# Batch norm's mean taken from column sums of the adjacency, in a four-layer graph network on one core

## The chip, the cores and the metric

The kernel runs on one core of a Trainium2 chip. The metric is the device time of one execution in microseconds. A core has five engines that each work through a list of instructions of their own: PE (matrix products), DVE (vector work), ACT (activations and copies), POOL (here mostly indirect DMAs, which gather or scatter rows by a list of indices) and SP (here only DMA issues). They wait for each other by semaphores.

## What is computed

The inputs are x, 2708 nodes with 128 features, and adj, 2708 x 2708 with about 0.6% of its entries set and a full diagonal. Four layers follow each other; around each there is a residual sum and a layer norm.

```python
# layer 0
msg = adj.T @ x
inv_deg = 1.0 / adj.sum(axis=0)            # 0 where that is infinite
x = layernorm(x + msg * inv_deg[:, None])
# layer 1
s = x @ msg_w[:, :D].T;  d = x @ msg_w[:, D:].T
messages = gelu(s[:, None, :] + d[None, :, :] + msg_b)
aggregated = einsum('ijd,ij->id', messages, adj)
new = concatenate([x, aggregated], -1) @ upd_w.T + upd_b
x = layernorm(x + layernorm(gelu(new) + x) * ln_w + ln_b)
# layer 2
h = adj @ (x @ W) + b
mean = h.mean(axis=0);  var = ((h - mean) ** 2).mean(axis=0)
h = gamma * (h - mean) * rsqrt(var + EPS) + beta
x = layernorm(x + where(h >= 0, h, 0.2 * h))
# layer 3: attention with four heads over the neighbours, then a product with w
```

Layer 0 sums adj over its rows for each column. Layer 2's mean is a mean of h over the nodes.

## The kernel before, in words

**Blocks.** The nodes are cut into 22 blocks: 21 of P = 128 and one of 20. `quads()` (L324) groups them for vector work into five groups of four, one of one and the last of 20 rows.

**Layer 0 (L343 to L808).** `load(b)` (L392) brings the rows of a block of adj on SP's queue. `count_and_sum` multiplies them with x, which has a column of ones behind its 128 features, so that the accumulators `accs0` hold adj.T @ x and, in column D of each block, the column sum of adj (L406). Meanwhile DVE extracts up to 31 entries for each row (`extract`, L421). DVE's order in this part is written out by hand (`manual_schedule`, L343); the other engines' orders, and DVE's later, come from a scheduler that puts instructions in order by their dependencies and estimates of their time. Nodes are then ranked by their number of entries, so that blocks in ranked order have nodes of like count (`rank`, `perm`).

The column sums are copied into `deg` (L701 to L711), zeros are replaced and the reciprocal taken. The generator `layer0(b0, count, n)` (L719) then works on a group of blocks: it normalises x + msg/deg into slot 1 of the tile `dx`, [128, count, 2, 128] (L754), transposes it on PE, multiplies it by the second half of msg_w and copies the product into slot 0 (L773). `d_dram` gets slot 0 in natural order (L774, SP). `dx_dram` gets both slots, 256 floats for each node, scattered to the node's rank: one indirect DMA on POOL for each block (`scatter`, L253).

**Layers 1 and 2 (L812 to L1005).** A loop runs over TURNS (L974), the ranked blocks in a fixed order. In a turn, `own_row` (L818) loads the block's 256 columns of `dx_dram` into `x_s`, on SP's queue, one turn ahead (L821). `messages` (L827) transposes it (L832), copies it to `x_st` on ACT (L833), and makes the node's own term on PE (L834, L835). DVE adds that to slot 0 (L849), ACT takes the Gelu. Then POOL gathers neighbours' rows of d_dram, up to eight to a buffer of `msg`, of which there are five (L245, L856). DVE adds (L858), ACT takes the Gelu (L861), and DVE weighs and sums (L844, L846) into `parts`. `update` (L868) has products for the new features (L872, L881 to L883), ACT's Gelu, two layer norms that go between DVE and ACT, a scatter to x2_dram, a transposition (L899), and the product with layer 2's W, which is copied into `xw` (L904). `x_b`, x_s plus a bias, is made on DVE at L877. Beside these, `transposed` (L906) transposes blocks of adj on PE (L931), copies them on ACT (L936) and stores them to at_dram (L938, SP).

From turn 11 on, with two blocks to a turn, `layer2(k)` (L950) gathers 128 rows of at_dram by `perm` on POOL and adds 22 products into six PSUM banks `accs2`, one for each output block of 128 columns (L957). Block 20 and block 21 lie in the first half of bank 5; its columns 2D to 4D aren't used. The last block follows behind the loop.

**Batch norm (L1030 to L1080).** DVE adds b to each group from PSUM into `hb` (L1052); PE multiplies a matrix of ones with each block, which sums over the nodes into `ps_m` (L1054). Two small products of weights for layer 3 follow on DVE (`w_prod`, L1060 to L1062). The mean is a scaled copy of ps_m (L1065); DVE subtracts it from every group (L1069), ACT squares (L1070), PE sums the squares into `ps_v` (L1072), and `scale` is made of it (L1077 to L1080). `masks` (L1085) makes index masks for layer 3 on DVE. The normalise loop (L1118) then multiplies by scale (L1120), adds beta, goes through the leaky relu, the residual and the layer norm, and stores tables for layer 3.

**Layer 3 (L1174 to L1508)** gathers rows of those tables and works on DVE, PE and ACT in orders written out by hand.

Of the kernel before, what the change touches and what calls it, by code (L numbers as in the profile page):

```python
# [9 lines left out]
FP = mybir.dt.float32  # L10
AF = mybir.ActivationFunctionType
ALU = mybir.AluOpType
# [3 lines left out]
P = 128  # L16
N = 2708
D = 128
NFULL = N // P
NREM = N - NFULL * P  # L20
NBLK = NFULL + 1
# [64 lines left out]
def gnn_resnorm_kernel(  # L86
# [21 lines left out]
    nc = tc.nc  # L108

    const = ctx.enter_context(tc.tile_pool(name="const", bufs=1))  # L110
    ident = const.tile([P, P], FP, name="ident")
# [98 lines left out]
    lists_dram = tables.tile([NBLK * P, LW], FP, name="lists_dram")  # L210

    d_dram = tables.tile([NBLK * P, D], FP, name="d_dram")
    dx_dram = tables.tile([NBLK * P, 2 * D], FP, name="dx_dram")
    at_dram = tables.tile([NBLK * P, N], FP, name="at_dram")
    x2_dram = tables.tile([NBLK * P, D], FP, name="x2_dram")

# [20 lines left out]
    ones = keep.tile([P, P], FP, name="ones")  # L237
# [6 lines left out]
    def gather(dst, table, index):  # L244
        nc.gpsimd.indirect_dma_start(  # L245
            out=dst,
            out_offset=None,
            in_=table[0:N, :],
            in_offset=bass.IndirectOffsetOnAxis(ap=index, axis=0),
        )  # L250
# [73 lines left out]
    def quads():  # L324

        parts = [(b, 4) for b in range(0, 20, 4)] + [(20, 1), (21, 1)]
        return [(b, c, BLOCKS[b + c - 1][1]) for b, c in parts]
# [7 lines left out]
    with ExitStack() as layer:  # L335
# [373 lines left out]
        tails = work.tile([P, 4], FP, name="tails")  # L709
        nc.vector.tensor_copy(tails[0:NREM], accs0[1][0:NREM, 3 * (D + 1) : 3 * (D + 1) + 4])  # L710
        nc.vector.tensor_copy(deg[0:NREM, NFULL : NFULL + 1], tails[0:NREM, 3:4])  # L711
        nc.vector.tensor_scalar(zero, deg, 0.0, None, ALU.is_equal)
        nc.vector.tensor_tensor(deg, deg, zero, ALU.add)
        nc.vector.reciprocal(deg, deg)
# [4 lines left out]
        def layer0(b0, count, n):  # L719
            h = brief.tile([P, 4, D], FP, name="h0", bufs=5)  # L720
            sums = brief.tile([P, 4], FP, name="sums0", bufs=5)
            var = brief.tile([P, 4], FP, name="var0", bufs=5)
            for j in range(count):
                jb = b0 + j
                k, c0, f0, f1 = acc_parts(jb)[0]
                f1 = min(f1, D)
                two = f1 < D
                nc.vector.scalar_tensor_tensor(
                    h[0:n, j, 0:f1], accs0[k][0:n, c0 : c0 + f1], deg[0:n, jb : jb + 1],
                    xs[0:n, jb, 0:f1], ALU.mult, ALU.add,  # L730
                    **({} if two else {"accum_out": sums[0:n, j : j + 1]}),
                )
                if two:
                    nc.vector.scalar_tensor_tensor(
                        h[0:n, j, f1:D], tails[0:n, 0:3], deg[0:n, jb : jb + 1],
                        xs[0:n, jb, f1:D], ALU.mult, ALU.add,
                    )
                    nc.vector.tensor_reduce(sums[0:n, j : j + 1], h[0:n, j, :], AX.X, ALU.add)
            sums, v = sums[0:n, 0:count], var[0:n, 0:count]
            nc.vector.tensor_scalar(sums, sums, -1.0 / D, None, ALU.mult)  # L740
            for j in range(count):
                junk = small.tile([P, D], BF, name="ln_junk")
                nc.scalar.activation(
                    junk[0:n], h[0:n, j, :], AF.Square, bias=sums[:, j : j + 1],
                    accum_out=v[:, j : j + 1],
                )
            yield
            nc.vector.tensor_scalar(v, v, 1.0 / D, EPS, ALU.mult, ALU.add)
            nc.scalar.activation(v, v, AF.Sqrt)
            yield  # L750
            nc.vector.reciprocal(v, v)
            dx = brief.tile([P, count, 2, D], FP, name=f"dx{count}", bufs=3 if count > 1 else 2)
            for j in range(count):
                nc.vector.tensor_scalar(  # L754
                    dx[0:n, j, 1, :], h[0:n, j, :], sums[:, j : j + 1], v[:, j : j + 1],
                    ALU.add, ALU.mult,
                )
            w = (count - 1) * P + n
            yield
            pt = sums_ps.tile([P, 512], FP, name="pt_x1", tag="bank")  # L760
            for j in range(count):
                nc.tensor.transpose(
                    pt[:, j * P : j * P + n], dx[0:n, j, 1, :], ident[0:n, 0:n]
                )
            xt = brief.tile([P, 512], FP, name="xt1")
            nc.scalar.copy(xt[:, 0:w], pt[:, 0:w])
            pm = sums_ps.tile([P, 4, D], FP, name="pm_d", tag="bank")
            for j in range(count):
                nc.tensor.matmul(
                    pm[0:n, j, :], lhsT=xt[:, j * P : j * P + n], rhs=wd_t, start=True, stop=True  # L770
                )
            yield
            nc.scalar.copy(dx[0:n, :, 0, :], pm[0:n, 0:count])  # L773
            nc.sync.dma_start(  # L774
                d_dram[b0 * P : b0 * P + w, :].rearrange("(b p) w -> p b w", p=n),
                dx[0:n, :, 0, :],
            )
            while b0 + count > SPLIT and 1 not in known:
                yield
            for j in range(count):  # L780
                did = scatter(
                    dx_dram, rank[0:n, b0 + j : b0 + j + 1],
                    dx[0:n, j].rearrange("p t d -> p (t d)"),
                )
                for before in known[1:]:
                    tc.declare_no_dep(
                        did, before, query=mybir.DependencyQuery.ANY_SYNC,
                        reason="each row has a place of its own",
                    )
                known.append(did)  # L790
# [27 lines left out]
        def own_row(b):  # L818
            n = BLOCKS[b][1]
            x_s = mine.tile([P, 2, D], FP, name="x_s", bufs=3)  # L820
            nc.sync.dma_start(  # L821
                x_s[0:n],
                dx_dram[b * P : b * P + n, :].rearrange("p (t d) -> p t d", t=2),
            )
            return x_s

# [120 lines left out]
        gamma_row = row_on_all(keep, gamma, "gamma_row")  # L947
        beta_row = row_on_all(keep, beta, "beta_row")

        def layer2(k):  # L950

            b, n = TURNS[k], BLOCKS[TURNS[k]][1]
            at = ring.tile([P, N], FP, name="at_rows", tag="rows")
            gather(at[0:n, :], at_dram, perm[0:n, b : b + 1])
            for ib in range(NBLK) if k == 0 else ORDER:
                i0, m = BLOCKS[ib]
                nc.tensor.matmul(  # L957
                    accs2[ib // 4][0:m, (ib % 4) * D : (ib % 4 + 1) * D],
                    lhsT=at[0:n, i0 : i0 + m],
                    rhs=xw[0:n, b, :],  # L960
                    start=(k == 0 and ib % 4 == 0),
                    stop=(k == NBLK - 1 and ib in (3, 7, 11, 15, 19, 20)),
                )
# [66 lines left out]
    with ExitStack() as layer:  # L1030
# [14 lines left out]
        def broad(row, n, count):  # L1045
            return row[0:n].unsqueeze(1).to_broadcast((n, count, D))

        ps_m = own_ps.tile([P, 512], FP, name="ps_m", tag="own")
        ps_v = tail_ps.tile([P, 512], FP, name="ps_v", tag="tail")
        for b0, count, n in quads():  # L1050
            a = accs2[b0 // 4].rearrange("p (j d) -> p j d", d=D)[0:n, b0 % 4 : b0 % 4 + count]
            nc.vector.tensor_tensor(hb[0:n, b0 : b0 + count], a, broad(b_row, n, count), ALU.add)  # L1052
            for b in range(b0, b0 + count):
                nc.tensor.matmul(  # L1054
                    ps_m[:, 0:D], lhsT=ones[0:n, :], rhs=hb[0:n, b, :],
                    start=(b == 0), stop=(b == NBLK - 1),
                )
        for w, wa in ((w2_sb, w_a2), (w1_sb, w_a1)):
            prod = small.tile([P, HEADS, D], FP, name="w_prod")
            nc.vector.tensor_tensor(prod, w, a_all, ALU.mult)  # L1060
            nc.vector.tensor_reduce(wa, prod, AX.X, ALU.add)
            nc.vector.tensor_scalar(wa, wa, 0.01, None, ALU.mult)  # L1062
        mean = work.tile([P, D], FP, name="bn_mean")
        scale = work.tile([P, D], FP, name="bn_scale")
        nc.vector.tensor_scalar(mean, ps_m[:, 0:D], 1.0 / N, None, ALU.mult)  # L1065
        for b0, count, n in quads():
            h = hb[0:n, b0 : b0 + count]
            sq = small.tile([P, 4, D], FP, name="bn_sq")
            nc.vector.tensor_tensor(h, h, broad(mean, n, count), ALU.subtract)  # L1069
            nc.scalar.activation(sq[0:n, 0:count], h, AF.Square)  # L1070
            for j in range(count):
                nc.tensor.matmul(  # L1072
                    ps_v[:, 0:D], lhsT=ones[0:n, :], rhs=sq[0:n, j, :],
                    start=(b0 + j == 0), stop=(b0 + j == NBLK - 1),
                )
        sent = []
        nc.vector.tensor_scalar(scale, ps_v[:, 0:D], 1.0 / N, EPS, ALU.mult, ALU.add)  # L1077
        nc.scalar.activation(scale, scale, AF.Sqrt)
# [953 lines left out]
```

## Time and profile before

| what | value |
|---|---|
| unprofiled runs | 1609.47, 1605.33, 1604.46 us; median 1605.33 |
| profiled execution | 1957.99 us |
| its span | 1956.3 us |
| mean granted PE clock in it | 0.668 |
| layers 1 and 2 | 229.7 to 1053.2 us |
| batch norm's statistics | 1053.2 to 1072.4 us |
| normalise loop and layer 3 | 1072.4 us to the end |

All durations in the profile come from the one profiled execution, which was longer than the runs without a profile. Times are microseconds from the start of its span unless they are called ns. A line of a group of instructions reads: line of the kernel, engine, operation, output<-inputs, shapes, count, then a bar, busy us and mean ns of one, then a bar, the idle time of the engine just ahead of them and who ended it. A line of the timeline reads: start, length, engine, line, operation, count, and in brackets the idle time before it and who ended it. An engine's name with q (SPq, ACTq) is its issuing of DMAs, and PEld is PE's loading of weights. "issue" and "remote" stand for idle time that no data dependency on the page explains.

### The profile page before, as it was taken

The page shows a single profiled execution, that of the slowest core. Times are in us where ns is not written, and L with a number is a line of the kernel's source. Part 1 is how long each engine was busy: PE and PEld are TensorE (multiplying, and loading weights), DVE is VectorE, ACT ScalarE, POOL GpSimd, SP SyncE. Part 2 cuts the span into 40 slices and gives each one's busy share as a digit, 9 for nine tenths or more (in the row PEclk, how much of TensorE's full clock was granted, in tenths as well). Part 3 has the DMA queues.
Part 4 walks back from the last instruction along what each step waited for, and adds up shares of the span by engine and source line. Part 5 has one row for each costly group of instructions (what it writes and reads, how often), then busy time and mean ns, then how long its engine had stood idle before and what let it go on. Part 6 is the DMA issues. An engine that isn't in the chain of part 4 may idle for free. (4 is left out here: it accounts for less than half of the span.)

```text
span 1956.3 us, 23628 instructions
## 1 busy us (share of the span) xinstructions
PE 1248.6 (64%) x5771; PEld 866.9 (44%) x5771; DVE 1173.2 (60%) x4900; ACT 768.6 (39%) x3134; POOL 896.4 (46%) x996
## 2 busy tenths in 40 slices
PE   7972414443345564556585647888798888877884
PEld 7972313333234453445465313445444444444444
DVE  8999536763353533343346626677678777676773
ACT  3475424542222311111111414455455555455543
POOL 1002655555544445444430454555565556555430
PEclk9985655555555576666677755677677777677675
DMA  8541547765444624332331474766475665756530
GB/s 288 228 160 41 170 94 195 202 169 145 125 90 117 173 96 96 109 132 88 141 110 37 153 222 130 190 189 194 140 206 178 173 178 153 189 159 191 153 109 7
DMA packets 164926, 289.61 MB, mean 148 GB/s; under 512 B 46850, under 2 KB 118752, under 8 KB 157679
## 3 DMA queue, kind: packets, MB, share of 16 engines
q0 software_dynamic: 60496, 190.76, 34.4%
q1 hardware_dynamic: 96739, 92.56, 15.6%
q10 hardware_dynamic: 7544, 4.69, 0.9%
q8 instruction: 48, 0.79, 0.2%
q14 instruction: 99, 0.81, 0.1%
HBM read 242.50 MB, written 45.35 MB: 147 GB/s over the span
## 5 line engine op out<-in xcount | busy, mean ns | idle before, releaser
L245 POOL DMA_INDIRECT g<-t_dram,idx x400 | 402.2, 1005 | 310.8 <-issue 169.2
L245 POOL DMA_INDIRECT msg<-d_dram,idx x368 | 348.7, 947 | 272.1 <-issue 225.7
L1324 ACT ACTIVATE sum_junk<-g 126x128 bf16<-126x128 f32 (+3 forms) x1024 | 302.6, 298 | 142.3 <-issue 60.8
L1293 PE MATMUL z<-x,copies 32*126 32x512 f32 (+3 forms) x800 | 220.3, 917 | 60.7 <-DVE g L1490 33.9
L957 PE MATMUL acc<-x_nat,at_rows 128*128 128x128 f32 (+2 forms) x968 | 168.8, 335 | 64.5 <-issue 52.6
L931 PE MATMUL pt_a<-ident,rows 128*128 128x128 f32 (+2 forms) x475 | 119.0, 408 | 131.5 <-ACT at_sb L936 106.9
L1490 DVE TENSOR_TENSOR g<-g,z 126x1536 f32<-126x1536 f32 (+3 forms) x100 | 175.1, 1751 | 40.1 <-remote 25.4
L1324 ACT ACTIVATION_READ_ACCUMULATOR sum_junk<-g 126x1 f32 (+3 forms) x1024 | 193.5, 189 | 0.0
L957 PEld LDWEIGHTS acc<-x_nat,at_rows 128*128 128x128 f32 (+2 forms) x968 | 151.2, 240 | 78.8 <-issue 67.5
L1298 PE MATMUL z<-g,ident 126*126 126x512 f32 (+3 forms) x200 | 168.5, 937 | 0.1
L1370 PE MATMUL po_s<-wm,g 126*128 126x24 f32 (+6 forms) x800 | 124.7, 310 | 59.7 <-DVE wm L1357 53.8
L931 PEld LDWEIGHTS pt_a<-ident,rows 128*128 128x128 f32 (+2 forms) x475 | 86.4, 212 | 154.8 <-ACT at_sb L936 120.9
L1370 PEld LDWEIGHTS po_s<-wm,g 126*128 126x128 f32 (+3 forms) x800 | 120.8, 237 | 75.1 <-DVE wm L1357 63.8
L1316 DVE SCALAR_TENSOR_TENSOR g<-g,a_ps 126x1536 f32<-126x1536 f32 (+6 forms) x100 | 151.1, 1511 | 0.0
L406 PE MATMUL acc<-x_nat,rows 128*128 128x129 f32 (+3 forms) x1012 | 128.5, 288 | 25.9 <-DMA rows<-in_adj_dram 15.1
L406 PEld LDWEIGHTS acc<-x_nat,rows 128*128 128x128 f32 (+2 forms) x1012 | 122.9, 197 | 31.1 <-DMA rows<-in_adj_dram 16.1
L846 DVE SCALAR_TENSOR_TENSOR own<-msg,ls,own 128x128 f32<-128x128 f32 (+1 forms) x302 | 106.5, 353 | 37.4 <-remote 13.5
L1293 PEld LDWEIGHTS z<-x,copies 32*126 32x126 f32 (+3 forms) x800 | 65.3, 250 | 97.9 <-issue 54.2
L1308 DVE SCALAR_TENSOR_TENSOR g<-z,a 126x128 f32<-126x128 f32 (+3 forms) x400 | 92.0, 287 | 19.4 <-DMA g<-t_dram,idx 9.4
L431 DVE FIND_INDEX8 ci<-cv,rows 128x8 uint32<-128x247 f32 (+2 forms) x242 | 101.6, 420 | 0.0
L436 DVE MAX8 cv<-rows 128x8 f32<-128x247 f32 (+2 forms) x242 | 98.0, 411 | 2.2 <-POOL rows L396 2.2
L1298 PEld LDWEIGHTS z<-g,ident 126*126 126x126 f32 (+3 forms) x200 | 41.7, 261 | 122.1 <-issue 109.1
(293 smaller groups left out, 2084.0 us busy)
## 6 DMA issues: line engine op xcount, KB each, us to landing
rows<-in_adj_dram SPq DMA_DIRECT2D x34, 1354.0 KB
at_dram<-at_sb SPq DMA_DIRECT2D x105, 256.0 KB
g<-t_dram,idx POOLq DMA_INDIRECT x400
msg<-d_dram,idx POOLq DMA_INDIRECT x368
t_dram<-t_row SPq DMA_DIRECT2D x21, 256.0 KB
x_s<-dx_dram SPq DMA_DIRECT2D x21, 128.0 KB
at_dram<-at_sb SPq DMA_DIRECT2D x21, 64.0 KB
d_dram<-dx SPq DMA_DIRECT2D x5, 256.0 KB
```

Of the source, the lines that this page charges most:

```text
L245: nc.gpsimd.indirect_dma_start(out=dst, out_offset=None, in_=table[0:N, :], in_offset=bass.IndirectOffsetOnAxis(ap=index, axis=0),)
L406: nc.tensor.matmul(accs0[k][0:m, c0 : c0 + f1 - f0], lhsT=rows[0:n, j0 : j0 + m], rhs=x_nat[0:n, b, f0:f1], start=k not in started, stop=( ...
L431: nc.vector.max_index(out=ci[0:n, at], in_max=cv[0:n, at], in_values=rows[0:n, c0 : c0 + cw])
L846: nc.vector.scalar_tensor_tensor(to, m, v, last, ALU.mult, ALU.add)
L931: nc.tensor.transpose(pt[0:m, j, 0:n], rows[0:n, c0 : c0 + m], ident[0:n, 0:n])
L957: nc.tensor.matmul(accs2[ib // 4][0:m, (ib % 4) * D : (ib % 4 + 1) * D], lhsT=at[0:n, i0 : i0 + m], rhs=xw[0:n, b, :], start=(k == 0 and i ...
L1293: nc.tensor.matmul(z3[0:e, r, :] if r < 3 else z1[0:e], lhsT=copies[g][rows, j, :], rhs=own[b][1][rows, :], start=True, stop=r < 3, skip_g ...
L1298: nc.tensor.matmul(z1[0:e], lhsT=ident[0:e, 0:e], rhs=g4[0:e, 3, 0:HD], start=False, stop=True, skip_group_check=True,)
L1316: nc.vector.scalar_tensor_tensor(z, z, 0.0, a_ps[0:e].unsqueeze(1).to_broadcast((e, count, HD)), ALU.max, ALU.mult)
L1324: nc.scalar.activation(junk[0:e], g4[0:e, r, hd * D : (hd + 1) * D], AF.Identity, accum_out=sc[0:e, r, hd : hd + 1],)
L1370: nc.tensor.matmul(po[:, p0 * HEADS : (p0 + g) * HEADS], lhsT=g4s[i][0:e, r, HD : HD + D], rhs=wm[0:e, 4 * i + r, :, :], start=True, stop= ...
L1490: nc.vector.tensor_tensor(z, z, z3[0:e], ALU.add)
```

## The change

Batch norm's mean over nodes is obtained another way. The sum of adj @ (xW) over all its rows equals the column sums of adj times xW. The column sums are at hand in layer 0. The changed kernel keeps a copy of them before zeros are replaced, carries them as a 257th column of dx and dx_dram (written by POOL, a copy for each group), so that they come out in ranked order, and loads that column into `column_sum`, [128, 22], with two DMAs on SP's queue ahead of the first `x_s`. In `layer2(k)`, ACT scales a 128 x 128 matrix of ones by the block's column sums (`weighed`, one buffer), and PE multiplies it with the block's xw into columns 2D to 3D of bank 5; so after the last block every partition of these columns holds the sum of h over nodes without the bias. In batch norm, the mean is that sum over N plus b, `shift` is b minus the mean, and one pass adds shift to the accumulators; the 22 products into ps_m and the pass that subtracts the mean are gone. The weights' products for layer 3 stand behind that pass.

```diff
-    dx_dram = tables.tile([NBLK * P, 2 * D], FP, name="dx_dram")
+    DX = 2 * D + 1
+    dx_dram = tables.tile([NBLK * P, DX], FP, name="dx_dram")
...
+        column_sums = work.tile([P, 24], FP, name="column_sums")
+        nc.vector.tensor_copy(column_sums, deg)
...
-            dx = brief.tile([P, count, 2, D], FP, name=f"dx{count}", bufs=3 if count > 1 else 2)
+            dx = brief.tile([P, count, DX], FP, name=f"dx{count}", bufs=3 if count > 1 else 2)
...
-            nc.scalar.copy(dx[0:n, :, 0, :], pm[0:n, 0:count])
+            nc.scalar.copy(dx[0:n, :, 0:D], pm[0:n, 0:count])
+            nc.gpsimd.tensor_copy(
+                dx[0:n, :, 2 * D : DX], column_sums[0:n, b0 : b0 + count].unsqueeze(2)
+            )
...
                 x_s[0:n],
-                dx_dram[b * P : b * P + n, :].rearrange("p (t d) -> p t d", t=2),
+                dx_dram[b * P : b * P + n, 0 : 2 * D].rearrange("p (t d) -> p t d", t=2),
...
+        column_sum = keep.tile([P, NBLK], FP, name="column_sum")
+        for b0, b1, n in ((0, NFULL, P), (NFULL, NBLK, NREM)):
+            nc.sync.dma_start(
+                column_sum[0:n, b0:b1],
+                dx_dram[b0 * P : b0 * P + (b1 - b0 - 1) * P + n, 2 * D : DX].rearrange(
+                    "(b p) o -> p (b o)", p=n
+                ),
+            )
...
             gather(at[0:n, :], at_dram, perm[0:n, b : b + 1])
+            weighed = small.tile([P, P], FP, name="weighed", bufs=1)
+            nc.scalar.activation(
+                weighed[0:n], ones[0:n], AF.Copy, scale=column_sum[0:n, b : b + 1]
+            )
             for ib in range(NBLK) if k == 0 else ORDER:
                 i0, m = BLOCKS[ib]
+                if ib == 21:
+                    nc.tensor.matmul(
+                        accs2[5][:, 2 * D : 3 * D], lhsT=weighed[0:n], rhs=xw[0:n, b, :],
+                        start=False, stop=False,
+                    )
...
-        ps_m = own_ps.tile([P, 512], FP, name="ps_m", tag="own")
+        shift = work.tile([P, D], FP, name="bn_shift")
+        nc.vector.scalar_tensor_tensor(
+            mean, accs2[5][:, 2 * D : 3 * D], 1.0 / N, b_row, ALU.mult, ALU.add
+        )
+        nc.vector.tensor_tensor(shift, b_row, mean, ALU.subtract)
         for b0, count, n in quads():
-            nc.vector.tensor_tensor(hb[0:n, b0 : b0 + count], a, broad(b_row, n, count), ALU.add)
-            for b in range(b0, b0 + count):
-                nc.tensor.matmul(
-                    ps_m[:, 0:D], lhsT=ones[0:n, :], rhs=hb[0:n, b, :],
-                    start=(b == 0), stop=(b == NBLK - 1),
-                )
+            h = hb[0:n, b0 : b0 + count]
+            sq = small.tile([P, 4, D], FP, name="bn_sq")
+            nc.vector.tensor_tensor(h, a, broad(shift, n, count), ALU.add)
+            nc.scalar.activation(sq[0:n, 0:count], h, AF.Square)
...
-        nc.vector.tensor_scalar(mean, ps_m[:, 0:D], 1.0 / N, None, ALU.mult)
-        for b0, count, n in quads():
-            nc.vector.tensor_tensor(h, h, broad(mean, n, count), ALU.subtract)
-            nc.scalar.activation(sq[0:n, 0:count], h, AF.Square)
```

## The prediction on record

> **What bounds the kernel now.** I read the page's totals first, then its chain of waits, then a table of busy time by stage, and only then the groups of instructions and the timeline of the places the diff touches.
>
> ```profile
> span 1956.3 us, 23628 instructions
> PE 1248.6 (64%) x5771; PEld 866.9 (44%) x5771; DVE 1173.2 (60%) x4900; ACT 768.6 (39%) x3134; POOL 896.4 (46%) x996
> POOL out_dram L253 0%; POOLq L1990 0%
> ```
>
> No engine is above 64% of the span, so the kernel is bound by waits between engines. The chain names only the last piece, so it can't say which wait matters, and I go by stage. The table's columns are the window, its length, busy time (and instructions) of PE, PE's weight loads, DVE, ACT and POOL, the granted PE clock, the DMA share and GB/s. The rows are layers 1 and 2 interleaved (two rows), the batch-norm statistics, its normalise loop, and layer 3.
>
> ```profile
> 229.70:682.40 452.70, 187.46 (x738) 144.61 (x737) 222.18 (x1052) 163.87 (x336) 232.26 (x244) 0.53 0.57 148
> 682.40:1053.20 370.80, 218.27 (x1206) 188.03 (x1206) 140.80 (x601) 50.35 (x137) 168.02 (x177) 0.68 0.32 105
> 1053.20:1072.40 19.20, 11.21 (x91) 10.29 (x89) 19.00 (x58) 5.35 (x9) 1.54 (x9) 0.93 0.31 87
> ```
>
> Only the third row has a full engine: DVE is busy 19.00 of 19.20 us, so work taken off DVE there shortens the kernel. In the second row nothing is full: PE works 218 of 371 us, and the largest waits there are in round trips (PE waits 31.9 us for ACT's x_st ahead of L834, and 28.4 us for DVE's x_n ahead of L899; DVE waits 85.4 us for ACT ahead of L889). What lengthens one leg of such a trip is paid by the turn.
>
> In the statistics stage, by groups (busy us and mean ns after the bar) and the timeline:
>
> ```profile
> L1052 DVE TENSOR_TENSOR hb<-acc,b_row 128x512 f32<-128x512 f32 x5 | 3.1, 684 | 9.0 <-PE acc L957 9.0
> L1069 DVE TENSOR_TENSOR hb<-hb,bn_mean 128x512 f32<-128x512 f32 x5 | 3.1, 686 | 0.0
> L1080 DVE TENSOR_TENSOR bn_scale<-bn_scale,gamma_row 128x128 f32<-128x128 f32 x1 | 0.3, 272 | 0.0
> 1059.39 0.29 DVE L1065 TENSOR_SCALAR bn_mean<-ps_m 128x128 f32<-128x128 f32 x1 [0.16 <-PE ps_m L1054]
> 1059.80 3.48 DVE L1069 TENSOR_TENSOR hb<-hb,bn_mean 128x512 f32<-128x512 f32 x7
> ```
>
> DVE adds the bias for 3.1 us and a little, then runs other work, takes the mean, and spends 3.48 us subtracting it.
>
> **What the Trainium skill says.** "VectorE: DVE Perf Modes", section "Why PSUM operands drop a tier", puts an fp32 operation with a PSUM operand at its plain rate. The trace agrees that this costs nothing extra here: 684 ns reading accumulators, 686 ns in place. So adding a shift from PSUM costs what adding the bias costs. "DMA: Bandwidth & Descriptors", section "Rules for kernel authors", says that a strided last dimension becomes one descriptor per element. The trace agrees: the diagonal of adj, read in the same shape as the new column_sum, holds a queue for 13.32 us (below). "Perfetto Trace Analysis", section "Tensor Engine Instruction (MATMUL, LD_WEIGHTS)", says that ACT, DVE and GpSimd are strict FIFO. So an instruction that waits on ACT holds everything behind it; the trace shows nothing against this.
>
> **The change, part by part.** The profiled execution took 1957.99 us, its span 1956.3 with 1.69 around it, 22% above the median 1605.33 of the unprofiled runs. The pieces below are absolute durations from it; I add them to the median, and the 22% error on a sum of 10 us is 2 us, inside the range.
>
> (1) *Statistics.* Out go seven subtractions, 3.48 us, and 22 ps_m products, which PE had hidden under DVE. The mean stays (one instruction of 0.29, now with the bias), and one shift is added, 0.27. The adds stay. After the last block of layer 2 one more product stands ahead of the end: the last block is 44 records in 6.87 us, 0.156 each, two for each product, 0.31. The DVE's first instruction now also must finish before the first add: a gap of about 0.2 for mean and shift each at the stage's start, where before an add started at once. Sum: -3.48 + 0.27 + 0.31 + 0.4 = -2.5. All DVE work before the first multiplication by scale stays in its order, so a scale that is ready earlier (squares can start some 4 us sooner) brings no more; if those squares and products did set some of the stage, up to -4.
>
> (2) *Column sums on their way in.* One DVE copy of 128x24 and seven POOL copies into dx. Five stand ahead of POOL's first scatter to dx_dram, where POOL idles 25.7 us; two stand among the scatters, which follow each other every 1.27 us from 197.3 to 226.9. Each at some 0.3 (the nearest small DVE rows): +0.6, between 0 and 1. A scatter row of 1028 bytes for 1024, and rows no longer at multiples of 1024: no row of the trace prices it; 4 bytes in 1024 of 22 scatters is 0.4%, so I take 0 and leave 1 for the upper end.
>
> (3) *column_sum's two DMAs.* They stand on SP's queue directly ahead of the first two x_s loads, behind the same scatters. 2688 and 20 pieces of four bytes. The trace has this very shape once, the diagonal, on ACT's queue:
>
> ```profile
> 16.27 13.32 ACTq L669 DMA_DIRECT2D diag<-in_adj_dram  x1
> 30.65 0.20 ACT L525 COPY lists<-diag 128x7 f32<-128x7 f32 x1 [10.67 <-DMA diag<-in_adj_dram]
> ```
>
> So SP is held 13.3 us at 231.8, and behind it stand x_s, at_dram stores and row loads. Before:
>
> ```profile
> 231.83 0.78 SPq L821 DMA_DIRECT2D x_s<-dx_dram  x2
> 240.32 0.29 DVE L877 TENSOR_TENSOR x_b<-x_s,lnb 128x128 f32<-128x128 f32 x1 [1.61 <-DMA x_s<-dx_dram]
> 274.96 0.94 POOL L245 DMA_INDIRECT msg<-d_dram,idx  x1 [0.30 <-issue]
> 292.35 0.94 POOL L245 DMA_INDIRECT msg<-d_dram,idx  x1 [16.45 <-issue]
> ```
>
> x_s would come 13 us later, and x_b on DVE and the first transposition on PE wait for it, with the extraction queued behind them on DVE. Against that: POOL gathers into its five msg buffers until 275.9 without needing x_s, and DVE reaches the use of x_s at L849 only at 269.13, 29 us after x_b, with gaps of 2 to 7 us that no data explains. Those gaps may take up the delay. If they do, 0; if not, 13.3 and POOL's wait of 16.45 grows by it. I take +5.
>
> (4) *Layer 2.* Each block gets a scaled copy on ACT, weighed, and one product. Price of the copy: the row L916, the same operation and shape, 407 ns; 22 of them 9.0 us, in a stage where ACT works 50 of 371. Products: 22 x 0.31 = 6.8 us of PE. Neither engine is full, so the work itself is hidden; the waits are not. There is one weighed buffer: the next copy waits on ACT until PE has used the last, and behind it on ACT stand ln_junk, x_st, agg_t and the message Gelus. In the order of instructions of the changed kernel, the second weighed product of a pair of blocks moves from the fifth pair on right behind the block ahead of it, before the L872 and L834 products of the turn. There PE waits for ACT, which first needs PE's earlier product. That round trip is about an ACT start, 0.41, and a PE product, 0.31, with crossings of 0.2 each (DVE's wait for the last ps_m product was 0.16): 1.1 us, in ten turns 11. Half of it meets PE or ACT idle anyway: +6, between 0 and 15 (a wait of ACT behind DVE's rstd in each turn). The mean of 28.4/12 = 2.4 us that PE waits at L899 could cover all of it.
>
> (5) *Moves.* w_prod, reduce and scaling go behind the adds on DVE; nobody needs them until the t_dram products: 0.
>
> Sum: -2.5 + 0.6 + 5 + 6 = +9.1, so 1605.3 + 9.1 = 1614.4.
>
> **The rivals.** *Everything is covered.* The gaps take up (3) and idle engines take up (4): -2.5 + 0.6 = -1.9, 1603.4. For it: DVE's unexplained gaps, PE at 59% in the second row. Against it: DVE, ACT and POOL serve in order, so a wait at the head is a wait of all behind.
>
> *Everything is exposed.* -2.5 + 1 + 13.3 + 15 = +27, 1632. For it: DVE's 85.4 us of waiting for ACT at L889 says that ACT's place in a turn counts. Against it: both can't well be on one path in full.
>
> *Faster, by a DMA pause at the start of layer 1.* Between 240 and 282 all engines but POOL crawl without a data reason, while row loads, at_dram stores and gathers share the DMA engines. If SP, held for 13 us, issues its large stores and loads later, DVE may reach L849 sooner than 269.13; the chain from there (L849, Gelu at 275.72, POOL's release at 292.35) then comes forward. It can give at most what DVE idles without reason between 256 and 269, 7.01 + 2.31 + 1.62 = 10.9; half is 5.5. With (1) and (2), and (4) covered: -1.9 - 5.5 = -7.4, 1597.9. It decides if L849 starts before about 264.
>
> *The change doesn't do what it says.* The ps_m products and subtractions are gone from the instruction list, so it does; only their worth can fail.
>
> **How the numbers follow.** Sum with half exposed 0.42 (1610 to 1622), all exposed 0.18 (to 1632), covered 0.20 (1601 to 1605), faster by the pause 0.20 (1596 to 1600). A measurement of this kernel can tell about 0.3%, 4.8 us, from no change. So slower 0.42 + 0.18 = 0.60, same 0.20, faster 0.20. The range takes in the half of the fast case that lies nearest, and all but the end of the slowest: 1598 to 1630.
>
> **What would show it.** (1): the adds at about 0.68 each, no group of subtractions, the stage near 16.7 us. (2): dx scatters still 1.27 apart but for two. (3): column_sum on SP's queue near 13 us, and x_b about 13 us later; if L849 is not later, the covered case holds. (4): PE's idle ahead of the weighed product in the second row: 0.6 us a turn is my sum, 1.5 the worst. Wrong it would be if the second row grew by over 20 us, or if a stage that the diff doesn't touch, layer 3, moved by more than 5.

## The result and the profile after

The changed kernel takes 1618.43 us (median of 10 runs, 1611.8 to 1622.62), the kernel before 1607.78 us (10 runs, 1604.46 to 1610.61). The ratio is 1.0073 with a 95% interval of 1.0054 to 1.0093: slower by 10.65 us, by the medians, where 9.1 was forecast. The sum came out; its terms, as the traces show below, did not.

One thing has to be known for all numbers that follow. Before takes 1608 us in the runs of the result and 1935 to 1951 us in those of all the experiments, a fifth more. The experiments ran on three chips; which chip ran the result is not on record, so that the chip makes the difference is likely, but not shown. I speak of runs of the first sort (1608) and of the second. The profile shown of before (1957.99 us) is of the second sort, the changed kernel's (1613.93 us, span 1612.1) of the first. So an experiment is compared only with runs of before on its own chip, and the changed kernel was run and profiled again on one of the second sort, as was before. The ratios with an interval leave out executions over 1.5% above the fastest of their kernel, the medians do not; the two part most for no copy on ACT, whose first set has one execution of 1909.00 us (0.9949 against 0.9988 by the medians) and whose second has one of 3043.76 us.

The statistics stage first. The stage's row of the table (window, length, busy time and instructions of PE, PE's weight loads, DVE, ACT, POOL, then PE clock, DMA share, GB/s), and its groups, in the profile of the changed kernel:

```profile
843.70:861.98 18.28, 7.29 (x45) 6.76 (x44) 15.79 (x54) 5.33 (x9) 1.50 (x9) 0.77 0.31 91
```

```profile
L1087 DVE TENSOR_TENSOR hb<-acc,bn_shift 128x512 f32<-128x512 f32 x5 | 3.1, 681 | 0.0
L1079 DVE SCALAR_TENSOR_TENSOR bn_mean<-acc,b_row 128x128 f32<-128x128 f32 x1 | 0.3, 292 | 9.6 <-PE acc L983 9.6
L1100 DVE TENSOR_SCALAR bn_scale<-ps_v 128x128 f32<-128x128 f32 x1 | 0.3, 290 | 2.5 <-PE ps_v L1090 2.5
L1082 DVE TENSOR_TENSOR bn_shift<-b_row,bn_mean 128x128 f32<-128x128 f32 x1 | 0.3, 289 | 0.0
```

The subtractions are gone, and the adds at 681 ns cost what they cost before. DVE's work falls from 19.0 to 15.79 us. The stage falls from 19.20 only to 18.28, because the third row of the groups is new: DVE stands idle for 2.5 us ahead of scale, until PE has summed the squares. Before, it came to that instruction late and found ps_v ready. The timeline of the changed kernel shows where the two meet:

```profile
844.50 3.46 DVE L1087 TENSOR_TENSOR hb<-acc,bn_shift 128x512 f32<-128x512 f32 x7
847.89 1.27 DVE L1096 TENSOR_TENSOR w_prod<-w_s,a_all 128x512 f32<-128x512 f32 x2
...
850.61 0.27 DVE L1120 TENSOR_SCALAR copies<-row_of,first 128x128 f32<-128x128 int32 x1
853.37 0.29 DVE L1100 TENSOR_SCALAR bn_scale<-ps_v 128x128 f32<-128x128 f32 x1 [2.49 <-PE ps_v L1090]
853.58 1.06 DVE L1120 TENSOR_SCALAR copies<-row_of,first 128x128 f32<-128x128 int32 x5
854.55 0.15 DVE L1129 TENSOR_SCALAR_CACHE_REDUCE after<-start 128x4 f32<-128x4 int32 x1
```

The scheduler put scale among the copies of the first mask. Behind it in DVE's order stand the rest of the masks, which need nothing of it, and they wait with it.

PE's side of the wait has changed too. These are its products that sum the squares, before and after:

```profile
1061.20 5.24 PE L1072 MATMUL ps_v<-bn_sq,ones 128*128 128x128 f32 x42 [1.85 <-ACT bn_sq L1070]
845.90 6.72 PE L1090 MATMUL ps_v<-bn_sq,ones 128*128 128x128 f32 x42 [2.12 <-ACT bn_sq L1088]
```

The same 42 records take 1.5 us longer. From about 846.8 to 850.2 us the granted PE clock is 0.50; before, it stays at 1.00 all through these products. By this difference I estimate that 1.5 of the 2.49 us come from PE being slower, and one from DVE being early.

Next, the start of layer 1: SP's queue, and the first x_b on DVE.

```profile
232.13 1.75 SPq L959 DMA_DIRECT2D column_sum<-dx_dram  x2
234.24 0.81 SPq L828 DMA_DIRECT2D x_s<-dx_dram  x2
```

```profile
236.55 0.29 DVE L884 TENSOR_TENSOR x_b<-x_s,lnb 128x128 f32<-128x128 f32 x1 [7.46 <-DMA x_s<-dx_dram]
```

column_sum holds SP for 1.75 us, not 13.3, and x_b starts at 236.55, no later than in any profile of before but one (236.04).

Last, the weighed products. The waits of ACT in layers 1 and 2 (us in total, times, longest), and two pairs of products on PE:

```profile
ACT weighed L972 <- PE acc L979: 34.6, 13, 11.0
```

```profile
718.85 0.39 PE L979 MATMUL acc<-x_nat,weighed 128*128 128x128 f32 x2
719.82 0.46 PE L979 MATMUL acc<-x_nat,weighed 128*128 128x128 f32 x2
...
782.97 0.39 PE L979 MATMUL acc<-x_nat,weighed 128*128 128x128 f32 x2
784.05 0.39 PE L979 MATMUL acc<-x_nat,weighed 128*128 128x128 f32 x2
```

The products of these two pairs start 0.97 and 1.08 us apart, which is what the forecast gave a round trip through ACT (1.1). But PE isn't idle in between: it has other products to do (from 719.17 and from 783.29), and in this whole profile it has no idle time ahead of any weighed product. The 0.6 us a turn that the forecast expected there are 0. What waits is ACT. Whether that costs the kernel anything is another matter. POOL's timeline from 560 to 840 us, those of its instructions that waited over half a microsecond:

```profile
579.98 1.00 POOL L255 DMA_INDIRECT x_dram<-x_n,perm  x1 [16.87 <-DVE x_n L321]
631.72 0.94 POOL L247 DMA_INDIRECT msg<-d_dram,idx  x1 [1.79 <-ACT x_nat L911]
778.49 1.00 POOL L255 DMA_INDIRECT x_dram<-x_n,perm  x1 [3.00 <-DVE spread L603]
793.53 0.91 POOL L255 DMA_INDIRECT x_dram<-x_n,perm  x1 [1.55 <-DVE own L853]
816.83 1.00 POOL L255 DMA_INDIRECT x_dram<-x_n,perm  x1 [12.38 <-DVE own L853]
834.40 0.97 POOL L255 DMA_INDIRECT x_dram<-x_n,perm  x1 [16.57 <-DVE x_n L321]
```

From 581 to 775 us there is one, of 1.79. But for it POOL issues an instruction of 0.94 us every 1.25 us there, and the turns go at its pace. The longest waits of a weighed copy, 10.98 us at 667.48 and 10.19 at 694.20, lie in just that stretch. In the first, PE sits idle for 11.58 us until gathered rows land at 655.62, then works on products with them for 11.54 us, and ACT waits for those; POOL doesn't stop for it. So I expect round trips to cost little before the last turns, where POOL has slack and then runs out of work. Four copies start behind 778 us (783.46, 784.47, 809.69, 827.33).

### The profile page after: what moved, and what is told of

Same layout as the page of the kernel before. It is cut to its first block, busy times and chain, and to the rows that moved or that the text cites. A ratio compares the mean times of both kernels' runs of the same rounds, so it can differ in the third digit from the quotient of the medians.

```text
span 1612.1 us, 23672 instructions
## 1 busy us (share of the span) xinstructions
PE 1158.9 (72%) x5771; PEld 812.4 (50%) x5771; DVE 1162.6 (72%) x4895; ACT 771.1 (48%) x3156; POOL 893.1 (55%) x1003
## 3 DMA queue, kind: packets, MB, share of 16 engines
q1 hardware_dynamic: 99473, 92.57, 18.9%
## 5 line engine op out<-in xcount | busy, mean ns | idle before, releaser
L247 POOL DMA_INDIRECT g<-t_dram,idx x400 | 398.0, 995 | 194.2 <-issue 113.8
L247 POOL DMA_INDIRECT msg<-d_dram,idx x368 | 349.2, 949 | 132.5 <-issue 112.3
L1316 PE MATMUL z<-x,copies 32*126 32x512 f32 (+3 forms) x800 | 212.7, 866 | 26.3 <-DVE g L1513 25.4
L983 PE MATMUL acc<-x_nat,at_rows 128*128 128x128 f32 (+2 forms) x968 | 148.0, 314 | 74.2 <-DMA at_rows<-at_dram,perm 73.1
L938 PE MATMUL pt_a<-ident,rows 128*128 128x128 f32 (+2 forms) x475 | 113.5, 396 | 117.2 <-ACT at_sb L943 116.5
L983 PEld LDWEIGHTS acc<-x_nat,at_rows 128*128 128x128 f32 (+2 forms) x968 | 134.1, 220 | 85.2 <-DMA at_rows<-at_dram,perm 69.9
L1321 PE MATMUL z<-g,ident 126*126 126x512 f32 (+3 forms) x200 | 158.4, 885 | 8.8 <-DMA g<-t_dram,idx 8.8
L1393 PE MATMUL po_s<-wm,g 126*128 126x24 f32 (+6 forms) x800 | 113.1, 294 | 31.8 <-DVE wm L1380 30.0
L1393 PEld LDWEIGHTS po_s<-wm,g 126*128 126x128 f32 (+3 forms) x800 | 109.2, 217 | 47.0 <-DVE wm L1380 41.7
L433 DVE FIND_INDEX8 ci<-cv,rows 128x8 uint32<-128x247 f32 (+2 forms) x242 | 97.8, 404 | 0.0
```

The source lines that it names most:

```text
L247: nc.gpsimd.indirect_dma_start(out=dst, out_offset=None, in_=table[0:N, :], in_offset=bass.IndirectOffsetOnAxis(ap=index, axis=0),)
L433: nc.vector.max_index(out=ci[0:n, at], in_max=cv[0:n, at], in_values=rows[0:n, c0 : c0 + cw])
L938: nc.tensor.transpose(pt[0:m, j, 0:n], rows[0:n, c0 : c0 + m], ident[0:n, 0:n])
L983: nc.tensor.matmul(accs2[ib // 4][0:m, (ib % 4) * D : (ib % 4 + 1) * D], lhsT=at[0:n, i0 : i0 + m], rhs=xw[0:n, b, :], start=(k == 0 and i ...
L1316: nc.tensor.matmul(z3[0:e, r, :] if r < 3 else z1[0:e], lhsT=copies[g][rows, j, :], rhs=own[b][1][rows, :], start=True, stop=r < 3, skip_g ...
L1321: nc.tensor.matmul(z1[0:e], lhsT=ident[0:e, 0:e], rhs=g4[0:e, 3, 0:HD], start=False, stop=True, skip_group_check=True,)
```

## The experiments

All ran where before takes 1935 to 1951 us. Two of the kernels were run in two sets, on two chips; their ratios came out 0.5% apart (0.2 and 0.4% by the medians), more than their intervals say. I don't read a cause from a difference below 0.5% (10 us) here. The stages are far steadier: the statistics stage took 19.20 us in each of three profiles of before.

**Before and after again.** Unchanged kernels.

> The kernel before, unchanged, for a second profile: the first one was 22% longer than the runs without a profile. 1607.8 us expected by every theory, and a profiled span within 1% of it. In it, layers 1 and 2 should end some 8 to 15 us earlier, measured from the first message gather, than in the changed kernel if the loss lies in them.

> The kernel before once more, for a profile that can be laid beside the changed kernel's. The runs of the two sets so far took about 1936 us on the chip they had, where the runs of the result took 1608. Either 1605 to 1612 or 1925 to 1955, by the chip.

> The changed kernel, unchanged, beside the experiments. Every theory that puts the loss into waits between engines expects 0.5 to 0.9% slower than before; if a chip shows no loss here, the loss depends on how fast its engines get on elsewhere.

Measured: before 1944.85 and 1946.74 us in single runs, on two chips. After 1936.70 us on the first of them, 1.0000 of before there (0.9973 to 1.0028). So the loss of 0.73% isn't there on this chip. The statistics stage's gain is: 19.20 us before, 18.20 after, with DVE's same 2.49 us ahead of scale. In the changed kernel column_sum holds SP for 5.16 us, and x_b starts at 240.24 us; before, it starts at 236.04 on the same chip and at 239.87 on the other:

```profile
239.87 0.29 DVE L877 TENSOR_TENSOR x_b<-x_s,lnb 128x128 f32<-128x128 f32 x1 [6.91 <-DMA x_s<-dx_dram]
```

```profile
240.24 0.29 DVE L884 TENSOR_TENSOR x_b<-x_s,lnb 128x128 f32<-128x128 f32 x1 [6.31 <-DMA msg<-d_dram,idx]
```

The first line is of before on the other chip, the second of after. So x_b can come some 4 us later. I had said that layers 1 and 2 would show the loss; from the first gather to the stage they took 800.5 us before (1032.6 less 232.1) and 800.5 after on the first chip, and 818.0 before on the other (1050.5 less 232.5), so on these chips they don't.

**Carrying alone.** The kernel before, with the wider rows, POOL's copies and the two loads, but neither the products nor the one pass:

```diff
+            nc.gpsimd.tensor_copy(
+                dx[0:n, :, 2 * D : DX], column_sums[0:n, b0 : b0 + count].unsqueeze(2)
+            )
...
+            nc.sync.dma_start(
+                column_sum[0:n, b0:b1],
```

> The kernel before, and in addition the column sums carried through dx and dx_dram and loaded into column_sum, which nothing reads. Theory (the loss is ACT's and PE's coupling by the weighed copies in layer 2): within 2 us of before. Rival A (the loss is in the carrying: POOL copies on the scatters' path, rows of 1028 bytes, SP held ahead of x_s): 6 to 12 us slower than before.

> The kernel before with the column sums carried and loaded and nothing else, once more. Where before takes about 1608 us, the theory expects 0.999 to 1.002 of before and rival A 1.004 to 1.008. Where before takes about 1936 us, 0.997 to 1.001 as in the first set.

Measured: 1934.49 us, 0.9985 (0.9959 to 1.0010), and on another chip 1941.86 us, 0.9940 (0.9909 to 0.9971). Neither is slower. Rival A, 6 to 12 us for the carrying, falls here. In the two profiles column_sum held SP for 8.10 and 5.35 us. With the 8.10, x_b started only at 249.05 us, and the kernel was no slower for it.

**One pass alone.** The changed batch norm in the kernel before. The true mean is left out; a row of an accumulator stands in its place.

```diff
         nc.vector.scalar_tensor_tensor(
-            mean, accs2[5][:, 2 * D : 3 * D], 1.0 / N, b_row, ALU.mult, ALU.add
+            mean, accs2[5][:, 0:D], 1.0 / N, b_row, ALU.mult, ALU.add
         )
```

> The kernel before, with the changed batch norm alone: one pass that adds a shift, no ps_m products, no subtraction; nothing carried, no weighed products. Left out: the true mean (a row of an accumulator stands in its place). By my sum of the statistics stage: 2.5 to 3.5 us faster than before by every theory; if it isn't faster, the stage's gain is lost to what follows it (rival B).

Measured: 1934.07 us, 0.9988 (0.9964 to 1.0011). By time alone this can't be told from nothing or from 3 us. The stage tells it; first its row in this kernel, then in the kernel before on the same chip:

```profile
1031.50:1049.70 18.20, 7.25 (x45) 6.76 (x44) 15.71 (x52) 5.33 (x9) 1.51 (x9) 0.76 0.32 91
```

```profile
1032.60:1051.80 19.20, 11.16 (x89) 10.26 (x88) 19.05 (x60) 5.34 (x9) 1.54 (x9) 0.94 0.30 87
```

DVE's work falls by 3.3 us and the stage by 1.0. So the gain is 1.0 us with or without the weighed products. The PE clock of the rows falls with it, from 0.94 to 0.76: PE's squares take 6.73 us for 5.25. That goes through all the profiles: over the 8 us from the first of these products the clock is 1.00 in the five that still have the products into ps_m, 0.79 in eight of those without them and 0.65 in five round trips. So the changed batch norm brings the lower clock. Which part of it does (the missing 22 products, the earlier squares, the DMA traffic that now runs beside them) no run separates.

**No copy on ACT.** The 22 products stay, but their first operand is read from column_sum with a stride of zero:

```diff
-            weighed = small.tile([P, P], FP, name="weighed", bufs=1)
-            nc.scalar.activation(
-                weighed[0:n], ones[0:n], AF.Copy, scale=column_sum[0:n, b : b + 1]
-            )
...
-                        accs2[5][:, 2 * D : 3 * D], lhsT=weighed[0:n], rhs=xw[0:n, b, :],
+                        accs2[5][:, 2 * D : 3 * D],
+                        lhsT=column_sum[0:n, b : b + 1].to_broadcast((n, P)), rhs=xw[0:n, b, :],
```

> The changed kernel, with the product's first operand a column of column_sum read 128 times in place of a copy that ACT scales; the 22 extra products, the carrying and the one pass stay. Theory (coupling by ACT's copies): 6 to 12 us faster than the changed kernel, so 1606 to 1612. Rival A (carrying): within 2 us of the changed kernel. Rival C (the PE products themselves, 22 times 0.3 us): within 3 us of the changed kernel.

> The changed kernel without the copy on ACT, once more. Where before takes about 1608 us, the theory (coupling by ACT's copies) expects 1604 to 1611, that is 0.994 to 1.002 of before, and rival A (carrying) 1.005 to 1.009. Where before takes about 1936 us, the first set gave 0.995 and the theory expects 0.993 to 1.000 again.

Measured: 1933.94 us, 0.9949 (0.9911 to 0.9988), and on another chip 1952.42 us, 0.9997 (0.9976 to 1.0019). The first ratio would agree with the theory, but the medians of the same runs stand at 0.9988; the second shows nothing. With after itself at 1.0000 on the first chip there was no loss to take away. Undecided.

**More buffers.** `bufs=1` becomes `bufs=4` for weighed.

> The changed kernel with four weighed buffers in place of one, so that ACT's copy doesn't wait until PE has used the last one. In the trace of the changed kernel ACT idled 34.6 us in 13 places ahead of such copies, for PE. Theory (coupling by ACT's copies): 4 to 10 us faster than the changed kernel. Rival A (carrying) and C (PE's products): the same as the changed kernel within 2 us.

Measured: 1937.49 us, 1.0013 (0.9984 to 1.0041), the same as the changed kernel (1.0000). A miss for the theory where before takes 1936 us: ACT's wait for PE to free the buffer costs nothing that can be measured there.

**Five round trips.** The copy and the product are made five times for each block; the sum is divided by five.

```diff
+                    for _ in range(5):
+                        weighed = small.tile([P, P], FP, name="weighed", bufs=1)
...
-            mean, accs2[5][:, 2 * D : 3 * D], 1.0 / N, b_row, ALU.mult, ALU.add
+            mean, accs2[5][:, 2 * D : 3 * D], 0.2 / N, b_row, ALU.mult, ALU.add
```

> The changed kernel with copy and product made five times for each block instead of once (one weighed buffer; the mean divides by five), so 88 more round trips between ACT and PE, of about 1.1 us each in the trace of the changed kernel (two products of a pair stand 0.97 to 1.23 us apart where nothing else comes between them). Theory (the loss of the result is these round trips, half exposed): about 48 us more than the changed kernel where before takes 1608 us, and, if the round trips matter where before takes 1936 to 1950 us too, as much there: 1.02 to 1.03 of before. Rival D (where before takes 1936 to 1950 us, the engines' idle time without a data reason takes the round trips up): below 1.008 of before there.

Measured: 1982.46 us, 1.0247 (1.0200 to 1.0293) of before, 1935.35. Rival D falls: round trips do cost there too, when five stand in a row. Against after's 1.0000, on another chip, 88 more trips cost 2.47% of 1935, 47.8 us, 0.54 us each: half of 1.1. Where, the stages say: from the first gather of at_rows to the last, 355.1 us against 339.4 in the changed kernel; from the last gather to the statistics, 63.9 against 37.1. More than half of the cost lies behind the last gather. The split is rough: four products of the block ahead have slipped behind that gather here (1020.59 to 1024.45). The end of it, on PE:

```profile
1074.12 0.39 PE L980 MATMUL acc<-x_nat,weighed 128*128 128x128 f32 x2
1074.34 0.28 PE L1051 MATMUL pw<-odd_sum,ones 128*128 128x1 f32 x2
1075.05 0.49 PE L980 MATMUL acc<-x_nat,weighed 128*128 128x128 f32 x2 [0.43 <-ACT weighed L977]
1076.04 0.49 PE L980 MATMUL acc<-x_nat,weighed 128*128 128x128 f32 x2 [0.49 <-ACT weighed L977]
1077.02 0.49 PE L980 MATMUL acc<-x_nat,weighed 128*128 128x128 f32 x2 [0.49 <-ACT weighed L977]
1077.99 0.79 PE L980 MATMUL acc<-x_nat,weighed 128*128 128x128 f32 x2 [0.49 <-ACT weighed L977]
```

A product every 0.98 us, with nothing beside it but the waits for ACT: the price of a round trip.

**Masks first.** To take away the new wait, DVE's order in the stage is written out by hand: the first mask ahead of scale, the second ahead of the reciprocal.

```diff
+        hand.enter_context(tc.manual_schedule(engines={engine.DVE}))
...
-        for g in KINDS[:3]:
-            masks(g)
+        masks(KINDS[0])
+        nc.vector.tensor_scalar(scale, ps_v[:, 0:D], 1.0 / N, EPS, ALU.mult, ALU.add)
+        nc.scalar.activation(scale, scale, AF.Sqrt)
+        masks(KINDS[1])
+        nc.vector.reciprocal(scale, scale)
+        nc.vector.tensor_tensor(scale, scale, gamma_row, ALU.mult)
+        masks(KINDS[2])
+        hand.close()
```

> The changed kernel with DVE's order in the statistics stage written out by hand: the first mask stands ahead of the instruction that makes scale out of ps_v, where DVE stood idle for 2.49 us, the second ahead of the reciprocal. By the stage's own lines: that idle time goes, the stage falls from 18.3 us to about 16, and the kernel is 2 to 2.5 us faster than the changed one. If the stage isn't shorter, DVE's work and not the wait was its bound.

> Both edits: no copy on ACT (the product reads a column of column_sum 128 times) and the masks ahead of scale. Theory: the sum of both, so 2 to 2.5 us below the kernel without the copy and 8 to 14 us below the changed kernel, and so 2 to 4 us below the kernel before.

Measured: 1946.27 us, 1.0052 (1.0027 to 1.0078), and with no copy on ACT 1945.22 us, 1.0026 (1.0000 to 1.0052). The stage did what was expected, and the kernel did not. The stage, then scale in it, then a line of the normalise loop behind it, in the kernel with the masks first:

```profile
1040.40:1056.80 16.40, 7.26 (x45) 6.76 (x44) 15.84 (x46) 5.34 (x9) 1.52 (x9) 0.80 0.35 101
```

```profile
1051.71 0.28 DVE L1137 TENSOR_SCALAR bn_scale<-ps_v 128x128 f32<-128x128 f32 x1
```

```profile
1103.77 0.51 DVE L1117 TENSOR_SCALAR copies<-row_of,first 128x120 f32<-128x120 int32 x2 [4.08 <-POOL row_of L1110]
```

The idle time ahead of scale is gone and the stage is 1.8 us shorter (16.40 for 18.20); PE's squares are as slow as in the changed kernel (6.73 us), but hidden. From the first multiplication by scale to layer 3's first gather, however, it took 68.9 us in both these kernels, against 60.4 in the changed one on this chip and 59.1 to 65.5 in all the other profiles of the second sort. So 3.4 us at least were lost there. A part can be read: in the kernel of the line above, DVE waits 4.08 us for an index row that POOL makes behind the loop's scatters (2.1 us with no copy on ACT). The rest I have not traced; the loop's order on DVE has changed too. This edit has no version that beats both kernels, and no other run here clearly does.

## Why the prediction was right in the sum and wrong in its terms

(1) *Statistics, -2.5 forecast.* Measured -0.92 in the result's profile and -1.0 in three more kernels with the one pass on another chip (one pass alone, no copy on ACT, after again). DVE's own work fell by 3.2 us, as priced. What failed is the assumption that DVE's work ahead of the first multiplication by scale "stays in its order": scale's place on DVE moved. DVE now comes to it ahead of PE's sums, and 2.49 us of the gain turn into a wait. The mask work that had covered PE before stood behind it, and DVE takes its instructions in order, as the Trainium skill's "Perfetto Trace Analysis" says in "Tensor Engine Instruction (MATMUL, LD_WEIGHTS)"; the trace agrees, with five copies of the mask that need nothing of scale starting only at 853.58, behind it. The 22 products into ps_m, which the forecast took out at no price because PE had hidden them, may have mattered too: with the changed batch norm PE's clock falls while it sums the squares, by the estimate above 1.5 of the 2.49 us.

(2) *POOL's copies, +0.6, between 0 and 1.* Sized too small, by what can be read: the first scatter of dx starts at 196.6 to 199.0 us in the four profiles without the carrying and at 199.2 to 200.4 in the ten with it, the first message gather at 229.5 to 232.5 and at 231.4 to 237.6. By the means both are some 2 us later (197.4 and 199.5, 231.0 and 233.2), with spreads of 1.1 to 6.2 us among profiles of one kind.

(3) *column_sum, +5, at most 13.3.* Wrong. The step that failed is the price from the diagonal: the same shape and the same number of pieces held ACT's queue for 13.32 us while adj was streaming in, and SP's for 1.75 to 8.10 here. So the shape sets no fixed hold; what else the DMA engines do at the time may be what differs, but no run separates that. The rule of the Trainium skill that the forecast used ("DMA: Bandwidth & Descriptors", "Rules for kernel authors") speaks of the number of pieces and of no time, and the number was right: the hardware queue's packets go from 96739 before to 99473 after, 2734 more for 2708 pieces. x_b started on time in the result's profile, up to some 4 us late with a hold of 5.16 us, and at 249.05 with one of 8.10, without a loss that can be measured.

(4) *Round trips, +6, between 0 and 15.* One trip was sized rightly: 1.1 forecast, 0.98 measured with nothing beside it. Where it would be paid was wrong: in the result's profile PE never sits idle ahead of a weighed product. "Half exposed" fits added trips where before takes 1936 us, 0.54 each on average. For the 22 trips of the change, none was exposed there within the error (after at 1.0000, give or take 5 us), though in that kernel's second profile PE does wait for weighed, 17.6 us in two places.

Where the result's 10.65 us come from is therefore not settled. The terms that were seen are -0.9 for the stage, up to +2 from POOL's copies and nothing from x_b; some 10 us are left for layer 2's coupling and the moved order of PE and ACT. The coupling was my theory for nearly all of it, and the result's own profile speaks against that much: PE never waits for a weighed copy, and of ACT's waits only those of the four copies behind 778 us lie where POOL no longer sets the pace; at 1.1 us fully exposed they are 4.4 us. The five round trips agree about the place, with over half of their cost behind the last gather, but can't give the size for runs of the first sort. So the forecast's sum came out in part by luck, and 5 us or more stay unexplained. A profile of before among runs of the first sort would tell in which stage they arise; none was had, and neither was an experiment.

The forecast's signs of being wrong do not help: layers 1 and 2 from the first gather of at_rows took 376.5 us after and 370.0 to 378.7 before, on the second sort, and layer 3, from its first gather to the end, differs by 16.6 us between two profiles of before alone (826.1 and 809.5), so that a shift of 5 us can't be read.

Of the rivals, "faster by a DMA pause" has no support. Its sign came: L849, which started at 269.13 us in the profile shown of before, has its counterpart at 239.53 in the result's profile. Its gain didn't, and L849 starts at 241.0 and 243.5 in two more profiles of before and at 266.26 with the carrying alone, so the late start belongs to neither kernel. "Everything is covered" (1603.4) fits the runs of the second sort (1.0000), not the result. "Everything is exposed" (1632) fails with column_sum's 13.3 us.

## What to carry to other kernels

When work is taken off the engine that bounds a stage, look at what the next producer does by then: here DVE lost 3.2 us of work and 2.5 of them came back as a wait for PE, because one dependent instruction stood ahead of independent work and PE had become slower. A scaled copy on one engine for a product on another was a round trip of about a microsecond here; look in the trace whether the second engine idles ahead of the product before you charge for it. And a difference under one per cent holds for the runs it was measured in: here it was 0.73% in one group and nothing in another.

## What the runs showed of the hardware that I had not expected

The same program took 1608 us in one group of runs and 1935 to 1951 us in others, on three chips. Layers 1 and 2 took 610.5 us in the changed kernel's first profile and 800.5 in its second, with the same instructions; POOL's waits without a data reason ahead of message gathers were 112.3 us and 234.7 us in the two. The statistics stage took 18.28 and 18.20 us: it isn't touched. A read of some 2700 pieces of four bytes held its queue anywhere from 1.75 to 13.32 us. And with the changed batch norm PE, though it has fewer products to do, ran the squares' sums at a granted clock of 0.79 for 1.00, in nine profiles out of nine at 0.79 or less.
